# Hyperedge keys from one-hot matrix products, two node scores from one product, and the second node ordering made in layer 2

## The chip, the core and the metric

One core of a Trainium2 chip runs the whole program. The time is device microseconds (us) of one execution. The engines named below are TensorE (PE; its weight loads are listed apart as PEld), VectorE (DVE), ScalarE (ACT), GpSimd (POOL) and the queue of SyncE (SP), which issues most of the transfers.

## The reference

Four graph layers follow each other, each as `x = x + layer(relu(layernorm(x)))`, on `x` of 8 batches, 2048 nodes and 64 features, with one 2048x2048 matrix `adj` of zeros and ones. The change touches layer 0 and the preparation for layer 3:

```python
# layer 0 (h is the normalized input; H: 2048 nodes x 64 hyperedges, zeros and ones)
h = x @ W
s = leaky_relu(h @ a_node, 0.2)
alpha = softmax(where(H.T > 0, s, NEG), axis=-1)
agg = einsum('ben,bnf->bef', alpha, h)                      # one row per hyperedge
beta = sigmoid((h @ a_gn)[:, None, :] + (agg @ a_ge)[:, :, None])
all_he = elu(beta * h + (1 - beta) * agg)                   # one row per (hyperedge, node)
industry = einsum('nm,bmf->bnf', adj / deg, x @ W_ind)
g = einsum('bne,benf->bnf', softmax(where(H > 0, scores(elu(agg)), NEG)), all_he)
out = mix of industry and g by a two-way softmax
# layer 1: adj @ h and adj @ (adj @ h); layer 2: three times adj @ v with two small products
# layer 3 (graph attention over the neighbours that adj names)
e = adj * leaky_relu(e_src[:, None] + e_dst[None, :], 0.2)
h_prime = softmax(e) @ h
```

## The kernel before

Features stand as pairs of batches (4 pairs, `NP`), 128 nodes to a tile (16 tiles, `NT`), 512 nodes to a chunk (4 chunks, `NC`). Large SBUF areas are named slots, q0 to q9, of 16 KB a partition; who holds a slot decides when the next holder may write it. The source order of the instructions gives priorities, and a planner then fixes one order per engine from estimated times; each engine executes its own list strictly in that order. So a line that stands later in the source can run between earlier ones, but an instruction that waits holds up everything behind it on its engine.

`start` does the first layer norm, `h = x @ W` in both layouts (`h_t` by feature in q2 and q3, `h_n` by node in q4 and q5), and checks `adj`. `count_nodes` counts each node's hyperedges and neighbours, and writes both counts to DRAM (`degs`). A flag is then read, and a branch ends this part: nothing of what follows starts before it.

`layer0_pairs` follows. Nodes are ordered by how many hyperedges they have (fullest first), so that the j-th hyperedge of a node has to be worked on for few node tiles only.

- `hyperedge_keys` calls `sort_nodes` for that order. `sort_nodes` reads the counts back from DRAM, forms one class per count (`classes`, L340), counts with two small products (`pk`, `pb`), runs a prefix sum on VectorE (L412), gets each node's rank (L423), and inverts the ranks to an order with 16 steps of three VectorE instructions (L439, L443, L447) and a small product `pp` each. Then 16 indirect transfers of GpSimd (L498) fetch the rows of `H` in that order; they are transposed (L509), and a product with a triangle of ones gives `key`: for each hyperedge and node the running number of this hyperedge among the node's. Last, `sort_nodes` is called a second time, for the order by neighbours, which only layer 2's `neighbours` and layer 3 use.
- `aggregate` writes `h_n` to the DRAM table `h_rows` (L743), computes `h @ a_gn` with 128 TensorE instructions of two columns (`pb`, from L747) and writes that to `h_rows` as well (`hb`, L749 and L750). It computes the scores of `a_node` (`pl`, L759), loads `HT` to form `cap` (L767 to L769), and then for each of the four pairs: masked scores `logits` (L778), their maximum (L780), the exponential (L782), 16 transposes (L789), the product with `h_n` (`pa`), and a chain of small steps for the hyperedge's own scores. `logits` has two tiles, in q6 and q7, with two pairs each; `cap` and `score` are in q8, the fetched rows in q9.
- `x_ind` makes `x @ W_ind` as a high and a low part (L201, L202), nodes 0 to 1023 in q6 (high) and q8 (low), the others in q7 and q9.
- `adj_product` with `Pairs` then streams `adj` through TensorE and does the pairwise work beside it; `Pairs` fetches rows of `h_rows` by the order (L1738).

In layer 2 three products with `adj` are streamed; beside the first one `neighbours` finds each node's neighbours. It is a generator: `after` advances it once in every second step of the stream. It loads the order (L1473), fetches rows of `adj` (L1486) and works on them with VectorE instructions of 2048 elements (L1490, L1494, L1500, L1503). What is left of it is run before the third product.

Of the kernel before, what the change touches and what calls it, by code (L numbers as in the profile page):

```python
# [7 lines left out]
F = mybir.dt.float32  # L8
BF = mybir.dt.bfloat16

F12 = mybir.dt.float32r
I32 = mybir.dt.int32
# [7 lines left out]
P = 128  # L20
# [47 lines left out]

class Halves:
# [17 lines left out]
class Split:  # L87


    def __init__(self, slots, name):  # L90
        self.hi = Halves(slots, f"{name}_hi", ("q6", "q7"), True)
        self.lo = Halves(slots, f"{name}_lo", ("q8", "q9"), True)
        self.parts = self.hi, self.lo


class Kernel:
# [8 lines left out]
    def __init__(self, tc, ctx, a):  # L105
        self.tc, self.nc, self.a = tc, tc.nc, a
        self.flip = 0
        self.short = False
        self.consts = ctx.enter_context(tc.tile_pool(reuse_waits="tile", name="consts", bufs=1))

        dram = ctx.enter_context(tc.tile_pool(reuse_waits="tile", name="dram", bufs=1, space=bass.MemoryType.DRAM))
        self.xs = [
            [a["xT"][:, :, c * CW : (c + 1) * CW].rearrange("q p n -> p q n") for c in range(NC)]
        ]


        self.h_rows = dram.tile([N, ROW], F, name="h_rows")
        self.g_rows = dram.tile([N, NB * D], F, name="g_rows")
        self.degs = dram.tile([P, 2, NT], F, name="degs")
        self.orders = [dram.tile([P, 2, NT], I32, name=f"order{i}") for i in range(2)]  # L120


        self.f_rows = dram.tile([N, WIDE], F, name="f_rows")
        self.att_rows = dram.tile([N, NB * D], F, name="att_rows")
        self.rdeg = dram.tile([NT, P], F, name="rdeg")

        self.h_sums = [dram.tile([8, P, CW], F, name=f"sums{q}") for q in range(NP)]
        self.h_parts = [dram.tile([P, 3, N], BF, name=f"parts{q}") for q in range(NP)]
        for i in range(3):
            self.xs.append([dram.tile([P, NP, CW], F, name=f"x{i}_{c}") for c in range(NC)])  # L130
        self.setup()
# [211 lines left out]
    def count_nodes(self, pool, slots, adj_deg):  # L343


# [4 lines left out]
        deg = pool.tile([P, 2, NT], F, name="both_deg")  # L350
        nc.vector.tensor_reduce(deg[:, 0], hm, axis=AX.X, op=OP.add)
        nc.vector.tensor_copy(deg[:, 1], adj_deg)
        nc.sync.dma_start(self.degs, deg)
# [27 lines left out]
    def sort_nodes(self, w, ps, which, J, spare):  # L381

# [3 lines left out]
        deg = w.tile([P, NT], F, name="deg")  # L386
        nc.sync.dma_start(deg, self.degs[:, which])
        least = self.classes(w, deg, J)
# [9 lines left out]
        pk = ps.tile([P, K * NT], F, name="pk", tag="sort")  # L398
        self.mm(pk, ones, cls.rearrange(flat))
        pb = ps.tile([P, K * NT], F, name="pb", tag="sort")  # L400
# [4 lines left out]
        size = K * NT  # L405
        sums = [w.tile([P, left + size], F, name="sums"), spare[:, : left + size]]
# [19 lines left out]
        order = w.tile([P, 2, NT], I32, name="order")  # L426
        nc.vector.tensor_copy(order[:, 0], rank)

# [6 lines left out]
        linef, ownf = self.numbers(w, P)  # L435
        pp = ps.tile([P, 2 * NT], F, name="pp", tag="sort")
        for t in range(NT):
            here = w.tile([P, P], BF, name="here", bufs=2)
            nc.vector.tensor_scalar(  # L439
                here, linef, lowf[:, 1, t : t + 1], None, op0=OP.is_equal  # L440
            )
            ids = w.tile([P, 2, NT], BF, name="ids", bufs=2)
            nc.vector.tensor_scalar(  # L443
                ids[:, 0], linef[:, :NT], lowf[:, 0, t : t + 1], float(t), op0=OP.is_equal,
                op1=OP.mult,
            )
            nc.vector.tensor_scalar(  # L447
                ids[:, 1], linef[:, :NT], lowf[:, 0, t : t + 1], ownf, op0=OP.is_equal,
                op1=OP.mult,
            )  # L450
            self.mm(
                pp, here, ids.rearrange("p i t -> p (i t)"), start=t == 0, stop=t == NT - 1
            )
        perm = w.tile([P, 2, NT], F, name="permf")
        nc.vector.tensor_copy(perm.rearrange("p i t -> p (i t)"), pp)
# [4 lines left out]
        nc.sync.dma_start(self.orders[which], order)  # L460
        return order
# [24 lines left out]
    def hyperedge_keys(self, w, ps, slots, key):  # L486


        nc = self.nc
        both = slots.tile([P, 2, NT, 2 * D], F, name="twice", tag="q9")  # L490
        got = both[:, 0].rearrange("p t e -> p (t e)")
        got, spare = got[:, : NT * D], got[:, NT * D :]
        got = got.rearrange("p (t e) -> p t e", t=NT)
        order = self.sort_nodes(w, ps, 0, len(HELD) - 1, spare)

        twice = both[:, 1].rearrange("p t (s e) -> p t s e", s=2)
        for t in range(NT):
            nc.gpsimd.indirect_dma_start(  # L498
                got[:, t], None, self.a["H"],
                bass.IndirectOffsetOnAxis(ap=order[:, 1, t : t + 1], axis=0),  # L500
            )
        for i in range(2):
            nc.vector.tensor_scalar(twice[:, :, i], got, 0.0, None, op0=OP.is_gt)
        upto = self.upto(w)
        nc.vector.memset(upto[:D, D:], 0.0)
        for c in range(NC):
            pt = ps.tile([P, TC, P], F, name="pt", tag="sort")
            for i in range(TC):
                nc.tensor.transpose(  # L509
                    pt[:, i], twice[:, c * TC + i].rearrange("n s e -> n (s e)"), self.ident  # L510
                )
            mt = w.tile([P, CW], BF, name="mt", bufs=2)
            self.copy(mt, pt.rearrange("e i n -> e (i n)"))
            pc = ps.tile([P, CW], F, name="pc", tag="sort")
            self.mm(pc, upto, mt)
            nc.vector.tensor_mul(key[:, c * CW : (c + 1) * CW], pc, mt)
        self.sort_nodes(w, ps, 1, NEAR[1], spare)
        return order

    def start(self, pool, slots):  # L520

        nc, tc, a = self.nc, self.tc, self.a
        with tc.tile_pool(reuse_waits="tile", name="k00", bufs=1) as k:
# [48 lines left out]
    def x_ind(self, slots, k):  # L572
        w_ind = self.block_diag(k, self.a["W_ind"], "w_ind")
        x_ind = Split(slots, "x_ind")
        hn = self.h[0]
        with self.tc.tile_pool(reuse_waits="tile", name="x_ps", bufs=3, space=PSUM) as ps:
            for t in range(NT):
                pn = ps.tile([P, NP, P], F, name="pn")
                for q in range(NP):
                    self.mm(pn[:, q], hn(q)[:, t * P : (t + 1) * P], w_ind)  # L580
                self.split(x_ind, t, pn.rearrange("n q f -> n (q f)"))
        return x_ind
# [82 lines left out]
    def layer0_pairs(self, slots):  # L665
# [3 lines left out]
        with tc.tile_pool(reuse_waits="tile", name="k0", bufs=1) as k:  # L669
            fcw, av = self.scorer(k)  # L670
            ind = Halves(slots, "ind", ("q0", "q1"), False)
            with tc.tile_pool(reuse_waits="tile", name="k1", bufs=1) as k1:
# [6 lines left out]
                with (  # L679
# [3 lines left out]
                    self.hyperedge_keys(kw, kps, slots, key)  # L683
                    self.aggregate(slots, h_t, h_n, fcw, av, both, agg_hi, agg_lo)
                order = k1.tile([P, 2, NT], I32, name="order")
                nc.sync.dma_start(order, self.orders[0])
# [20 lines left out]
            order = k.tile([P, 2, NT], I32, name="order")  # L707
            nc.sync.dma_start(order, self.orders[0])
# [17 lines left out]
    def aggregate(self, slots, h_t, h_n, fcw, av, both, agg_hi, agg_lo):  # L726
        nc, tc, a = self.nc, self.tc, self.a
        with (
# [5 lines left out]
            agn = w.tile([P, 2], F, name="agn", bufs=1)  # L734
            node = w.tile([P, R], F, name="node", bufs=1)
            nc.vector.memset(agn, 0.0)
            nc.vector.memset(node, 0.0)
            for s in range(2):
                h = slice(s * D, (s + 1) * D)
                nc.vector.tensor_copy(agn[h, s : s + 1], self.col("a_gn")[h])  # L740
                nc.vector.tensor_copy(node[h, s : s + 1], self.col("a_node")[h])
            for t in range(NT):
                nc.sync.dma_start(self.h_rows[t * P : (t + 1) * P, : NB * D], h_n(t))  # L743
            pb = ps1.tile([P, NT, NB], F, name="pb", tag="pg")
            for t in range(NT):
                for q in range(NP):
                    self.mm(pb[:, t, 2 * q : 2 * q + 2], h_t(q)[:, t * P : (t + 1) * P], agn)  # L747
            hb = w.tile([P, NT, NB], F, name="hb", bufs=1)
            nc.vector.tensor_copy(hb, pb)  # L749
            nc.sync.dma_start(  # L750
                self.h_rows[:, NB * D :].rearrange("(t p) b -> p t b", p=P), hb
            )
# [3 lines left out]
            for ch in range(NC):  # L756
# [6 lines left out]
                )  # L763

            logits = [slots.tile([P, 2, N], F, name=f"logits{i}", tag=f"q{6 + i}") for i in range(2)]
# [6 lines left out]
            for q in range(NP):  # L772
                lg = logits[q // 2][:, q % 2]
# [55 lines left out]
                for s in range(2):  # L829
# [4 lines left out]
                    )  # L834
            flat = aggs.rearrange("p q s f -> p (q s f)")
# [535 lines left out]
    def layer2(self, slots):  # L1371
# [4 lines left out]
        with (  # L1376
# [41 lines left out]
            near = self.neighbours(k, slots) if self.short else iter(())  # L1418
# [48 lines left out]
    def neighbours(self, k, slots):  # L1467
# [5 lines left out]
        nc.sync.dma_start(order, self.orders[1])  # L1473
# [437 lines left out]
class Near:  # L1911
# [5 lines left out]
    def __init__(self, kern, slots, w, ps):  # L1917
# [15 lines left out]
        nc.sync.dma_start(self.order, kern.orders[1])  # L1933
# [323 lines left out]
```

## Time and profile before

| | |
|---|---|
| median of 3 runs | 2223.89 us (2223.14 to 2229.41) |
| the profiled execution | 2223.47 us, its span 2221.7 us |
| granted TensorE clock, mean | 0.905 |
| PE busy | 1967.9 us (89%) |
| DVE busy | 1115.2 us (50%) |
| ACT busy | 708.9 us (32%) |
| POOL busy | 727.9 us (33%) |

The span goes from the first to the last instruction of the profiled execution. Seen from its start, the first part ends at about 112 us with the branch; the keys and `aggregate` fill 112 to 270 us; the first product with `adj` and the pairs 270 to 484 us; the mix of layer 0 to 668 us; layer 1 to about 1385 us; layer 2 to about 1925 us; layer 3 the rest. Busy shares over the whole span average stages with different limits, so the stage from 112 to 270 us has to be read by itself. In lists of waits, "A <- B: 27.3, 1, 27.3" says that A stood idle 27.3 us in total, once, until B released it.

### The profile page before, as it was taken

The numbers are of one execution on the slowest core, as the hardware profiler recorded it, in microseconds if no ns is written. First come the engines' busy times: TensorE is split into PE (matmuls) and PEld (weight loads), VectorE is DVE, ScalarE is ACT, GpSimd is POOL, SyncE is SP. The second block draws the span as 40 slices with busy tenths as digits, with TensorE's granted clock in tenths as the row PEclk, the third lists the DMA queues.
The fourth block names the chain that finished last, engine by engine and source line by source line (L and its number), as shares of the span: only waits on it lengthen the run. The fifth ranks groups of instructions, "written<-read, shape, count | busy, mean of one in ns | idle before, by whom it ended". The sixth has DMA issues, their size and how long they took to land.

```text
span 2221.7 us, 21410 instructions
## 1 busy us (share of the span) xinstructions
PE 1967.9 (89%) x7530; PEld 1187.1 (53%) x7530; DVE 1115.2 (50%) x1980; ACT 708.9 (32%) x1347; POOL 727.9 (33%) x609
## 2 busy tenths in 40 slices
PE   5877899987879989999999998998999999679873
PEld 1454766652226766353353532876777666345432
DVE  7846767744762032524425244988302222349762
ACT  6401455543444342020110200433434333258300
POOL 0012066755320002726537175011000000277760
PEclk8856899996777989999999998999999999789996
DMA  8231133451122453040130402456333443375655
GB/s 318 71 101 27 52 94 112 126 159 67 38 76 86 131 130 118 0 139 13 54 99 0 114 1 82 149 191 218 103 123 123 144 151 124 131 199 164 180 158 201
DMA packets 107742, 253.76 MB, mean 114 GB/s; under 512 B 19600, under 2 KB 19744, under 8 KB 100320
## 3 DMA queue, kind: packets, MB, share of 16 engines
q1 hardware_dynamic: 90000, 185.22, 26.1%
q0 software_dynamic: 17616, 67.00, 10.1%
q8 instruction: 63, 1.03, 0.2%
q14 instruction: 63, 0.52, 0.1%
HBM read 218.37 MB, written 33.81 MB: 114 GB/s over the span
## 4 chain that ended last, share of the span: by engine, by line
PE 57%; DVE 8%; POOL 7%; DMA 6%; issue 5%; ACT 3%; SPq 1%; POOLq 0%; DVEq 0%; ACTq 0%
PE pp L135 25%; PE pk L135 16%; PE bank L135 4%; POOL ring L1959 3%; PE acc L135 3%; PE pn L135 2%; PE p L135 2%; POOL q L1794 1%; DVE q L1809 1%; DMA q<-in_adj_dram,order 1%; POOL dt L632 1%; DMA adj_t<-in_adjT_dram 1%; PE pd L135 1%; PE po L135 1%; DMA ring<-f_rows,near 1%
## 5 line engine op out<-in xcount | busy, mean ns | idle before, releaser
L294 ACT CAST adj<-adj_t 128x512 fp32r<-128x512 f32 x384 | 236.7, 619 | 718.3 <-PE pp L135 625.2
L1353 POOL TENSOR_TENSOR acc<-acc,y 128x512 f32<-128x512 f32 x224 | 277.4, 1271 | 444.9 <-DVE y L1348 444.9
L135 PE MATMUL pk<-q,w 128*128 128x512 f32 (+1 forms) x1024 | 358.2, 612 | 9.9 <-DVE w L1270 8.9
L135 PEld LDWEIGHTS pk<-q,w 128*128 128x128 f32 (+1 forms) x1024 | 136.6, 188 | 228.0 <-issue 179.1
L135 PE MATMUL acc<-q,ident 128*128 128x512 f32 x416 | 205.1, 620 | 30.0 <-DVE q L2049 19.1
L1348 DVE SCALAR_TENSOR_TENSOR y<-pk,bias,q 128x512 f32<-128x512 f32 x224 | 157.7, 746 | 139.9 <-PE pk L135 130.3
L135 PE MATMUL pp<-adj,u_n_hi 128*128 128x512 f32 x768 | 217.2, 402 | 0.0
L135 PE MATMUL pp<-adj,u_n_lo 128*128 128x512 f32 x768 | 214.2, 398 | 0.0
L135 PEld LDWEIGHTS pp<-adj,u_n_hi 128*128 128x128 f32 x768 | 143.4, 188 | 39.0 <-issue 5.9
L1959 POOL DMA_INDIRECT ring<-f_rows,near x121 | 141.4, 1169 | 69.2 <-issue 57.4
L135 PEld LDWEIGHTS pp<-adj,u_n_lo 128*128 128x128 f32 x768 | 144.6, 188 | 34.5
L135 PEld LDWEIGHTS acc<-q,ident 128*128 128x128 f32 x416 | 77.1, 196 | 106.3 <-issue 48.8
L2063 POOL IOTA q<- 128x2048 int32 x1 | 1.8, 1835 | 355.3 <-PE p L135 355.3
L1794 POOL TENSOR_TENSOR q<-q,beta 128x512 f32<-128x512 f32 x57 | 67.6, 1188 | 104.8 <-DVE beta L1770 81.6
L135 PE MATMUL pp<-adj,x_ind_hi 128*128 128x512 f32 x256 | 95.5, 489 | 2.1 <-DVE q L700 1.9
L1348 DVE SCALAR_TENSOR_TENSOR acc<-pk,bias,q 128x512 f32<-128x512 f32 x32 | 22.6, 746 | 143.6 <-PE pk L135 143.6
L135 PE MATMUL bank<-std,from_rows 32*128 32x512 f32 x128 | 47.7, 938 | 41.8 <-DVE std L242 33.8
L135 PE MATMUL pp<-adj,h_n_hi 128*128 128x512 f32 x256 | 77.7, 416 | 0.0
L135 PE MATMUL pp<-adj,h_n_lo 128*128 128x512 f32 x256 | 75.3, 407 | 0.0
L2030 DVE TENSOR_TENSOR q<-ring,e 128x1024 f32<-128x1024 f32 x58 | 69.9, 1217 | 9.9 <-PE acc L135 9.7
L135 PE MATMUL pp<-adj,ah_n_hi 128*128 128x512 f32 x256 | 73.1, 405 | 0.0
L1416 DVE TENSOR_TENSOR q<-pn,later 128x512 f32<-128x512 f32 x32 | 21.5, 687 | 101.6 <-PE pn L135 101.4
(382 smaller groups left out, 3216.7 us busy)
## 6 DMA issues: line engine op xcount, KB each, us to landing
adj_t<-in_adjT_dram SPq DMA_DIRECT2D x160, 512.0 KB, 3.8
rows<-in_adj_dram SPq DMA_DIRECT2D x16, 1024.0 KB, 5.6
adj_t<-in_adjT_dram SPq DMA_DIRECT2D x64, 256.0 KB, 3.0
q<-x SPq DMA_DIRECT2D x12, 1024.0 KB, 5.0
q<-in_embT_dram SPq DMA_DIRECT2D x8, 1024.0 KB, 12.2
x<-q SPq DMA_DIRECT2D x8, 1024.0 KB, 3.9
x_ch<-in_xT_dram SPq DMA_DIRECT2D x4, 1024.0 KB, 6.2
h_rows<-q SPq DMA_DIRECT2D x16, 256.0 KB, 2.9
```

The source lines that it names most:

```text
L135: self.nc.tensor.matmul(out, lhsT, rhs, start=start, stop=stop)
L294: nc.scalar.copy(moving, at[:, i])
L632: nc.gpsimd.tensor_sub(dt, th[0], th[1])
L1348: nc.vector.scalar_tensor_tensor(y, pks[b, half], bias[:, b : b + 1], emb[:, b], op0=OP.add, op1=OP.mult,)
L1353: nc.gpsimd.tensor_add(acc, acc, y)
L1416: nc.vector.tensor_add(to, pn, later[:, 2].unsqueeze(1).to_broadcast(full))
L1794: self.nc.gpsimd.tensor_tensor(x, x, by.unsqueeze(2).to_broadcast([P, NB, D]), op=OP.mult)
L1809: nc.vector.tensor_add(d, d, self.pas.pop(i - 1))
L1959: self.nc.gpsimd.indirect_dma_start(to, None, self.kern.f_rows[:], bass.IndirectOffsetOnAxis(ap=index, axis=0))
L2030: nc.vector.tensor_tensor(y.rearrange("n i (b f) -> n i b f", b=NB), block[:, i : i + 2, : NB * D].rearrange("n i (b f) -> n i b f", b=NB) ...
L2063: nc.gpsimd.iota(whole, pattern=[[1, N]], base=0, channel_multiplier=0)
```

## The change

The hyperedge counts stay in SBUF (`self.deg`), and the transfer to DRAM and back is gone. `sort_nodes` is split: `ranks` ends with the ranks, `by_rank` inverts them, now with whole-tile VectorE instructions (`here`, `place`, `ids`) followed by 16 products. `hyperedge_keys` no longer fetches rows: it loads `H` in node order with one transfer and, for each chunk of 512 places and each of 16 node tiles, makes a one-hot matrix (`hot`: which node has this rank) and multiplies. The products put the columns in order, so the transposes are gone too. It has become a generator, advanced once after each pair of `aggregate`; the order itself is made after the second pair.

`h @ a_gn` comes out of the same product as the scores of `a_node` (two more columns of `node`); the product is copied to `raw` by ScalarE, and after each pair four tiles of it are transposed and the wanted columns copied to `hb`, which is written to `h_rows` after the fourth pair. `logits` has one tile now, in q6, used by turns; `raw` and the rank's working space take q7; `x_ind`'s first nodes stand in q7 (high) and q9 (low).

The order by neighbours is made in layer 2, by `ranks` and `by_rank` at the head of `neighbours`, in the slot q4, with the PSUM banks called `p2`; it is written to DRAM for layer 3.

```diff
-        nc.sync.dma_start(self.degs, deg)
...
-    def sort_nodes(self, w, ps, which, J, spare):
+    def ranks(self, w, bank, which, J):
...
-        deg = w.tile([P, NT], F, name="deg")
-        nc.sync.dma_start(deg, self.degs[:, which])
-        least = self.classes(w, deg, J)
+        least = self.classes(w, self.deg[:, which], J)
...
+        return rank
+
+    def by_rank(self, w, bank, rank, order):
...
+        nc.vector.tensor_tensor(
+            here, line.unsqueeze(1).to_broadcast(full), lowf[:, 1].unsqueeze(2).to_broadcast(full),
+            op=OP.is_equal,
+        )
...
+        nc.vector.tensor_mul(ids[:, 0], place, tiles.unsqueeze(2).to_broadcast(full))
+        nc.vector.tensor_scalar(ids[:, 1], place, own, None, op0=OP.mult)
...
         for t in range(NT):
-            here = w.tile([P, P], BF, name="here", bufs=2)
-            nc.vector.tensor_scalar(
-                here, linef, lowf[:, 1, t : t + 1], None, op0=OP.is_equal
-            )
-            ids = w.tile([P, 2, NT], BF, name="ids", bufs=2)
...
+            self.mm(pp, here[:, t], ids[:, :, t], start=t == 0, stop=t == NT - 1)
...
-    def hyperedge_keys(self, w, ps, slots, key):
+    def hyperedge_keys(self, w, bank, both, rank, key):
...
-        order = self.sort_nodes(w, ps, 0, len(HELD) - 1, spare)
...
-        for t in range(NT):
-            nc.gpsimd.indirect_dma_start(
-                got[:, t], None, self.a["H"],
-                bass.IndirectOffsetOnAxis(ap=order[:, 1, t : t + 1], axis=0),
-            )
+        nc.sync.dma_start(got, self.a["H"].rearrange("(t p) e -> p t e", p=P))
...
+        line, _ = self.numbers(w, CW)
         for c in range(NC):
-            pt = ps.tile([P, TC, P], F, name="pt", tag="sort")
-            for i in range(TC):
-                nc.tensor.transpose(
-                    pt[:, i], twice[:, c * TC + i].rearrange("n s e -> n (s e)"), self.ident
+            here = w.tile([P, NT], F, name="rank_here", bufs=2)
+            nc.vector.tensor_scalar(here, rank, float(-c * CW), None, op0=OP.add)
+            pt = bank()
+            for t in range(NT):
+                hot = w.tile([P, CW], BF, name="hot", bufs=4)
+                nc.vector.tensor_scalar(hot, line, here[:, t : t + 1], None, op0=OP.is_equal)
+                self.mm(
+                    pt, twice[:, t].rearrange("n s e -> n (s e)"), hot, start=t == 0,
+                    stop=t == NT - 1,
                 )
...
             nc.vector.tensor_mul(key[:, c * CW : (c + 1) * CW], pc, mt)
-        self.sort_nodes(w, ps, 1, NEAR[1], spare)
-        return order
+            yield
...
-        x_ind = Split(slots, "x_ind")
+        x_ind = Split(slots, "x_ind", ("q7", "q6", "q9", "q8"))
...
-                    self.hyperedge_keys(kw, kps, slots, key)
-                    self.aggregate(slots, h_t, h_n, fcw, av, both, agg_hi, agg_lo)
-                order = k1.tile([P, 2, NT], I32, name="order")
-                nc.sync.dma_start(order, self.orders[0])
...
+                    rank = self.ranks(Parts(raw[:, 1]), bank, 0, len(HELD) - 1)
+                    keys = self.hyperedge_keys(kw, bank, twice, rank, key)
+                    for i, _ in enumerate(
+                        self.aggregate(slots, raw[:, 0], h_t, h_n, fcw, av, both, agg_hi, agg_lo)
+                    ):
+                        next(keys, None)
+                        if i == 1:
+                            self.by_rank(Parts(twice[:, 0]), bank, rank, order)
...
+                nc.vector.tensor_copy(node[h, 2 + s : 3 + s], self.col("a_gn")[h])
             for t in range(NT):
                 nc.sync.dma_start(self.h_rows[t * P : (t + 1) * P, : NB * D], h_n(t))
-            pb = ps1.tile([P, NT, NB], F, name="pb", tag="pg")
-            for t in range(NT):
-                for q in range(NP):
-                    self.mm(pb[:, t, 2 * q : 2 * q + 2], h_t(q)[:, t * P : (t + 1) * P], agn)
...
+                nc.scalar.copy(raw[:, s], pl)
+
+            logits = slots.tile([P, 2, N], F, name="logits", tag="q6")
...
+                g = q
+                pt = ps1.tile([P, 4, P], F, name="pt")
+                for i in range(4):
+                    t = 4 * g + i
+                    nc.tensor.transpose(pt[:, i], raw[:, t * P : (t + 1) * P], self.ident)
+                nc.vector.tensor_copy(
+                    hb[:, 4 * g : 4 * g + 4].rearrange("n i (q s) -> n i q s", s=2),
+                    pt.rearrange("n i (q c) -> n i q c", c=R)[:, :, :, 2:4],
+                )
+                yield
+            nc.sync.dma_start(
+                self.h_rows[:, NB * D :].rearrange("(t p) b -> p t b", p=P), hb
+            )
...
-        nc.sync.dma_start(order, self.orders[1])
+        w = Parts(slots.tile([P, 2 * N], F, name="sort", tag="q4"))
+        rank = self.ranks(w, bank, 1, NEAR[1])
+        yield
+        self.by_rank(w, bank, rank, order)
+        nc.sync.dma_start(self.order3, order)
+        yield
```

## The prediction

> **What bounds the kernel now.** I read the 40 slices of the page first. TensorE is nine tenths busy nearly everywhere, but in the third to fifth slice (111 to 278 us) it is not, and its granted clock is at half.
>
> ```profile
> ## 2 busy tenths in 40 slices
> PE   5877899987879989999999998998999999679873
> DVE  7846767744762032524425244988302222349762
> PEclk8856899996777989999999998999999999789996
> ```
>
> Then busy time in stretches of that stage. Columns: stretch, its length, then busy time and count of PE, PEld, DVE, ACT, POOL; then clock, DMA share, GB/s.
>
> ```profile
> 113.60:141.00 27.40, 27.40 (x129) 27.38 (x130) 0.17 (x2) 0.00 (x0) 0.00 (x0) 0.50 0.11 40
> 161.00:174.50 13.50, 13.50 (x28) 3.75 (x27) 8.79 (x10) 2.48 (x3) 10.76 (x10) 0.50 0.15 27
> 174.50:185.30 10.80, 0.09 (x2) 0.03 (x1) 1.75 (x4) 2.09 (x2) 8.06 (x10) 0.50 0.18 46
> 197.00:216.00 19.00, 16.75 (x98) 13.04 (x97) 16.25 (x39) 4.94 (x9) 0.29 (x1) 0.90 0.00 0
> 216.00:230.00 14.00, 8.19 (x40) 5.36 (x41) 13.10 (x57) 2.68 (x3) 0.00 (x0) 0.68 0.00 1
> 254.00:268.80 14.80, 12.62 (x111) 12.25 (x109) 11.52 (x39) 9.35 (x19) 0.00 (x0) 1.00 0.32 96
> ```
>
> The reader should see three holes: 27.4 us in which TensorE alone works, 10.8 us in which it does nothing while GpSimd issues fetches, and 216 to 230, where it idles half the time beside a full VectorE. The waits of 112 to 270 us, and those of the SP queue, name them:
>
> ```profile
> DVE hb L749 <- PE pb L135: 27.3, 1, 27.3
> PE pt L509 <- DVE twice L503: 10.7, 1, 10.7
> DVE twice L503 <- DMA twice<-in_H_dram,order: 9.1, 1, 9.1
> PE pp L135 <- DVE ids L447: 13.8, 28, 4.0
> SPq L387 <- DVE cls L391: 27.0, 1, 27.0
> ```
>
> So VectorE stands behind `hb` until the 128 small products end; the SP queue stands behind the second load of counts (L387) with 12 of 16 `h_rows` writes and both `HT` loads; TensorE later waits for fetched rows. Last, groups of VectorE and the stretches of layer 2:
>
> ```profile
> L439 DVE TENSOR_SCALAR here<-linef,lowf 128x128 bf16<-128x128 f32 x32 | 8.9, 278 | 0.7 <-PE pp L135 0.7
> L143 DVE COPY et<-pt 128x512 f32<-128x512 f32 x8 | 5.5, 688 | 3.4 <-PE pt L789 3.4
> 1411.00:1559.00 148.00, 139.41 (x616) 109.30 (x615) 132.62 (x95) 50.11 (x84) 21.30 (x13) 0.98 0.59 200
> 1572.00:1709.00 137.00, 136.77 (x615) 107.31 (x613) 13.33 (x20) 49.62 (x84) 0.00 (x0) 1.00 0.41 126
> ```
>
> **The change part by part.** All sums are against the profiled execution (2223.47 us, span 2221.7), 0.4 us under the median 2223.89: the same for this purpose. The stage begins at 113.6 and ends with the first product with `adj` at 269.8.
>
> *Up to the first masked scores (L778 at 167.2).* The 128 products (27.4 us) go. What is late next is `cap`: its mask (L768) starts at 161.26 as the second `HT` load lands. From the SP queue's resuming `h_rows` writes at 142.9 that took 18.4 us (12 writes of 0.61, two issues, 7.2 to land). Without the count loads the queue goes straight on: four writes (1.8 us) from 113.9, then 18.4, so L768 at about 134, L769, and L778 at 136.5 instead of 167.2. The scores are earlier: the 32 `pl` instructions take 8.9 us at half clock, to about 123, then the sign steps. Four ScalarE copies to `raw` (0.60 each) and one more load of `H` (0.43 us issue; the same load in the first part landed in 6.8) lie beside this. Ranks: 13 classes, eight additions of about 0.4 and the rest, some 8 us of VectorE, done near 125. **Gain 30.7.**
>
> *The hole at 174.5.* The 16 fetches (1.25 us apart on GpSimd, 160.7 to 182.3) and the wait on them go: **gain 10.7.** The load of `H` in node order replaces them 10 us before it is needed.
>
> *The middle, 185.3 to 254 (68.7 us).* Out: the second sort. VectorE: nine additions (4.0), at, rank, copies (3.5), 16 x 0.53 for the inversion (8.5), together 16 us; TensorE's idle half of 216 to 230 (5.8) and 16 transposes of rows (4.3). In: 64 one-hots and 64 products. The row for a one-hot is L439: started every 0.20 us for 128 columns, while L443 beside it, 16 columns, is started every 0.14; 112 columns cost 0.06, so 512 cost 0.20 + 384 x 0.06/112 = 0.40, 25.6 us for 64. [...] Some 20 of the 64 fit between 125 and 136.5, where VectorE would wait for `cap`; 44 are left, 17.6 us against 16 taken out. Inverting the first sort by whole tiles costs about 4 us instead of 8.5.
>
> On TensorE a product of 512 columns is started every 0.233 us at full clock (the stream's groups of four, 0.93 apart). [...] The trace shows 0.50 through 174.5 and 0.68 to 0.90 after 197. At 0.5 the 64 products cost 29.8 us, at full clock 14.9[...]. I take 0.8, 18.6, 44 of them here: 12.8. Four tiles of `raw` per pair add 16 transposes (2.4) and four short copies (1). TensorE: +15.2 - 4.3 - 3 (the second sort's `pp`) = +8, less the 5.8 of idleness. **Loss 2**, between a gain of 8 (warm clock: the 59 us of TensorE work here shrink) and a loss of 20 [...].
>
> *The tail, 254 to 269.8.* 80 of the 128 `x_ind` products lie here now, 48 before. With q7 under `raw` and q9 under the keys, none can start until the last transposes of `raw` and the last key product: 48 x 0.118 = 5.7 us more here, of which I let 3 come back in the middle. `hb` is now written at the end: copy 0.3, issue 0.6, landing 4.9, fetch 0.95 and 3.8, 10.5 us, beside 15.1 us of `x_ind` and 2.9 of `pb`. It costs nothing while these last; with no cover, up to 10. **Loss 3.**
>
> *Layer 2.* Sort and inversion come to 10 + 4.5 us of VectorE, and cannot start before 1385.2 (slot q4 is read until then). The neighbours' chain, with VectorE 90% busy to 1559 and ending at 1571.6, moves back by some 25 us; the third product, which needs it finished, begins at 1709: 137 us of cover. It needs 58 advances of the generator plus two; the stream offers 64. GpSimd's fetches wait behind the order, and nothing else is queued there. TensorE gets 18 small products (2 x 0.3, 16 x 0.19 = 3.6), and could stand behind the chain at two places, up to 10 us. No row shows this wait; the same products on TensorE's list waited 13.8 us in 28 pieces before because `ids` came one by one. **Loss 3**, between 1 and 14.
>
> The warm clock deserves a term of its own: pairs' `pl` (22.7 us for 32 instructions, mean 863 ns) run at 0.50 for the first two pairs; fewer holes should return **5**, between 0 and 10.
>
> Sum: 30.7 + 10.7 - 2 - 3 - 3 + 5 = 38.4. 2223.5 - 38.4 = 2185. The pairs, the mix, layer 1 and layer 3 have the same instructions, only earlier.
>
> **The rivals.** *The keys come last.* The source places chunk c after pair c; if the planner keeps them there, the early one-hots (8 us) are not early, chunk 3 (6.4 + 2) stands before `x_ind`, and nothing of the 5 or the 3 returns. That takes about 20: 2205. For it: the planner's order of the first sort left VectorE behind `hb` for 27 us. Against: in 145 to 160 it mixed two sorts well.
>
> *The stage becomes compact.* TensorE's work in it, at full clock, is 75 to 85 us; if the idle shares vanish, it ends 55 us earlier: 2168. For it: the 0.50 rows; against: the chain of each pair (a reduction of 2.3, an exponential of 2.2, transposes, small steps).
>
> *Lock step (slower).* Each product needs its one-hot and each one-hot a free buffer of four; with both engines strictly in order, a late instruction of the pair's chain stops both. [...] The gains without the keys' cost are 30.7 + 10.7 + 16 + 5 = 62, less 6 for tail and layer 2: 56. From 0.87 us per one-hot nothing is left[...]. Against: four buffers, and the `here` and `pp` of the first sort ran at VectorE's pace, 0.53 us, with no hand-over on top.
>
> *It does not do what it says* would be a fetch still waited for: the pairs still gather rows of `h_rows`, now behind `hb`; uncovered, that is 10 less gain, 2195, inside the range.
>
> **How the numbers follow.** The forecast with its bounds 0.68; keys last 0.15; compact 0.10; no change that can be measured 0.02; lock step 0.05. About 0.3%, 6.7 us, is what a measurement of this kernel can tell from none. Faster 0.93, same 0.02, slower 0.05. The range reaches from compact (2166) to keys last (2207).
>
> **What would show it.** Right: L778 first near 136; no wait of DVE on `pb` and no L498; 64 one-hots of about 0.48 us duration; first product with `adj` near 229; the neighbours' last L1507 near 1597, and the third product begun no later relative to layer 2's start than before plus 3. Wrong: one-hots of 0.7 us, TensorE waiting on `hot` by more than 10 us in sum, `x_ind` alone at the end for over 20 us, or a hole in layer 2's stream.

## The result, and the profile after

The changed kernel takes 2192.55 us (median of 5 runs, 2190.21 to 2206.33) against 2223.89: a ratio of 0.9868, 95% interval 0.9838 to 0.9898, some 31 us faster. The forecast was 2185, in a range of 2166 to 2207. The sign and the largest term were right; the gain is some 7 us smaller than the sum said.

Three rows of the 40 slices of the changed kernel, in tenths, as shown for the kernel before:

```profile
## 2 busy tenths in 40 slices
PE   5869999978879979999999998999999999679883
DVE  7877677725651133525434245898602222349772
PEclk8868999977759989999999998999999999789986
```

The granted clock of the third slice was 5 tenths and is 6, that of the fourth was 6 and is 8. TensorE's busy share in the third is still only six tenths. Busy time in stretches of this stage (columns: stretch, length, busy time and count of PE, PEld, DVE, ACT, POOL; clock, DMA share, GB/s):

```profile
113.60:141.00 27.40, 13.53 (x46) 3.40 (x47) 19.76 (x55) 4.51 (x8) 1.16 (x6) 0.62 0.69 214
123.00:135.00 12.00, 2.49 (x4) 0.58 (x4) 5.25 (x12) 1.34 (x3) 0.00 (x0) 0.61 0.80 205
135.00:148.00 13.00, 12.04 (x19) 3.88 (x21) 11.91 (x22) 3.38 (x3) 0.32 (x2) 0.50 0.00 1
148.00:165.00 17.00, 16.64 (x85) 10.14 (x85) 15.88 (x39) 4.81 (x9) 0.00 (x0) 0.90 0.00 1
165.00:185.00 20.00, 19.95 (x103) 12.06 (x103) 16.46 (x41) 4.47 (x9) 0.00 (x0) 0.76 0.00 1
185.00:204.00 19.00, 15.79 (x84) 10.22 (x84) 15.64 (x37) 5.04 (x9) 0.00 (x0) 0.86 0.00 0
217.00:238.00 21.00, 19.60 (x152) 19.14 (x152) 13.80 (x40) 11.70 (x22) 2.79 (x3) 0.90 0.46 155
```

Of the three holes of before, the one in which TensorE alone did small products and the one behind the fetches are gone. A new one stands at 123 to 135: TensorE does 2.5 us of work in 12 and VectorE 5.3, while the DMA engines are 80% busy. Then, up to 204, both engines are busy for eight tenths of the time or more. The waits of 112 to 217 us, and that of VectorE's one-hots in the groups of the stage (its line has the total busy time, the mean ns of one, then the idle time before and its releaser), say what for:

```profile
DVE cap L779 <- DMA cap<-in_HT_dram: 6.6, 1, 6.6
PE pl L153 <- DVE logits L789: 9.1, 1, 9.1
PE bank L153 <- DVE hot L519: 3.2, 2, 2.9
L519 DVE TENSOR_SCALAR hot<-linef,rank_here 128x512 bf16<-128x512 f32 x64 | 28.0, 481 | 2.6 <-PE bank L153 2.3
```

VectorE stands for `HT`, whose load is issued at 122.6, behind the 16 writes of `h_rows` (4 MB, issued from 113.4 on); TensorE stands for the masked scores. No wait on the small products or on fetched rows is left. VectorE's timeline over the hole (start, duration, what, [idle before]):

```profile
124.22 1.27 DVE L519 TENSOR_SCALAR hot<-linef,rank_here 128x512 bf16<-128x512 f32 x3
132.11 1.23 DVE L779 TENSOR_SCALAR cap<-cap 128x2048 f32<-128x2048 f32 x1 [6.62 <-DMA cap<-in_HT_dram]
134.69 1.29 DVE L789 TENSOR_TENSOR logits<-pl,cap 128x512 f32<-128x512 f32 x2
135.90 1.28 DVE L509 TENSOR_SCALAR twice<-twice 128x1024 bf16<-128x1024 f32 x2
```

Four one-hots are made before the hole (the first at 123.22) and none in it: the four buffers of `hot` are full, and no product can empty one, because the other factor, `twice`, is made from `H` only at 135.9. The load of `H` stands behind both loads of `HT` in the same queue: it is issued at 123.8 and takes 9.6 us to land, so it is not there before about 133.4 either. The end of the stage on TensorE (the last line is that of the kernel before):

```profile
216.62 16.91 PE L153 MATMUL pn<-w_ind,q 128*128 128x128 f32 x126
...
238.18 1.74 PE L153 MATMUL pp<-adj,x_ind_hi 128*128 128x512 f32 x4
...
269.76 1.91 PE L135 MATMUL pp<-adj,x_ind_hi 128*128 128x512 f32 x4
```

The first product with `adj` (the "stage end" from here on) begins at 238.2 instead of 269.8.

### The profile page after: what moved, and what is told of

It is laid out like the page before. It is cut to its first block, busy times and chain, and to the rows that moved or that the text cites. A ratio compares the mean times of both kernels' runs of the same rounds, so it can differ in the third digit from the quotient of the medians.

```text
span 2204.5 us, 21222 instructions
## 1 busy us (share of the span) xinstructions
PE 1961.8 (89%) x7461; PEld 1166.3 (53%) x7466; DVE 1135.3 (52%) x1964; ACT 713.0 (32%) x1351; POOL 709.2 (32%) x595
## 4 chain that ended last, share of the span: by engine, by line
PE 55%; DVE 11%; POOL 7%; issue 6%; DMA 5%; ACT 3%; SPq 1%; POOLq 0%; DVEq 0%; ACTq 0%
PE pp L153 23%; PE pk L153 16%; PE bank L153 4%; PE acc L153 3%; POOL ring L1991 2%; PE p L153 2%; PE pn L153 2%; DMA q<-in_adj_dram,order 1%; POOL q L1826 1%; DVE q L1841 1%; POOL dt L644 1%; DVE top L1532 1%; PE pd L153 1%; PE po L153 1%; PE pt L1252 1%
## 5 line engine op out<-in xcount | busy, mean ns | idle before, releaser
L1518 POOL DMA_INDIRECT q<-in_adj_dram,order x15 | 21.9, 1459 | 174.9 <-DVE top L1532 136.0
L2062 DVE TENSOR_TENSOR q<-ring,e 128x1024 f32<-128x1024 f32 x58 | 70.1, 1220 | 11.5 <-PE acc L153 11.3
```

Of the source, the lines that this page charges most:

```text
L1518: nc.gpsimd.indirect_dma_start(row, None, self.a["adj"], bass.IndirectOffsetOnAxis(ap=order[:, 1, t : t + 1], axis=0),)
L2062: nc.vector.tensor_tensor(y.rearrange("n i (b f) -> n i b f", b=NB), block[:, i : i + 2, : NB * D].rearrange("n i (b f) -> n i b f", b=NB) ...
```

## The experiments

All kernels ran in turn with the kernel before, which gave medians of 2223.7 to 2225.8 in these sets; a median here is that of 4 to 12 executions. The stage's end in the trace is the sharper measure: in the two profiles of the change it differs by 0.6 us, while from there to the end of the span the profiled executions took anything from 1946 to 1966 us with nearly the same instructions. Where the intervals of two kernels overlap, their medians alone do not tell them apart. That is so for e4_usort, e5_ukeys, e7_tmm and e8_half beside e1_again, for e9_fetch and e10_loads16 beside e2_loads, and for e12_smallloads beside e3_usmall.

| kernel | first masked scores | stage end | median, us | ratio to before (95%) |
|---|---|---|---|---|
| before | 167.2 | 269.8 | 2223.89 | |
| the change, first profile | 134.7 | 238.2 | 2192.55 | 0.9868 (0.9838 to 0.9898) |
| e1_again | 135.0 | 238.8 | 2191.55 | 0.9855 (0.9835 to 0.9876) |
| e2_loads | 128.2 | 229.2 | 2183.11 | 0.9810 (0.9786 to 0.9834) |
| e3_usmall | 157.4 | 260.3 | 2216.14 | 0.9959 (0.9941 to 0.9977) |
| e12_smallloads | 154.9 | 259.1 | 2210.09 | 0.9935 (0.9911 to 0.9959) |
| e4_usort | 139.4 | 243.3 | 2195.55 | 0.9868 (0.9847 to 0.9890) |
| e5_ukeys | 133.6 | 235.1 | 2189.92 | 0.9846 (0.9812 to 0.9880) |
| e6_thot | 133.6 | 260.2 | 2214.97 | 0.9957 (0.9940 to 0.9974) |
| e7_tmm | 133.7 | 237.8 | 2199.25 | 0.9872 (0.9838 to 0.9906) |
| e8_half | 132.8 | 236.4 | 2185.95 | 0.9834 (0.9805 to 0.9864) |
| e9_fetch | 128.0 | 221.0 | 2177.36 | 0.9791 (0.9770 to 0.9811) |
| e10_loads16 | 127.3 | 224.8 | 2177.77 | 0.9792 (0.9768 to 0.9816) |
| e11_best16 | 127.4 | 226.8 | 2185.90 | 0.9840 (0.9817 to 0.9863) |

**The change again.**

> The changed kernel unaltered, for a second profile. In the first, layer 1 (from the clock's dip at 1012 us to 1365) took 353 us against 345 before the change, with the same instructions. Theory 'a slow execution': layer 1 takes 345 to 347 here, the profiled execution is near 2195, the median 2190 to 2195. Rival 'the change slows layer 1': 352 to 354 again, and some 8 us of gain are still to be had.

From stage end to the head of layer 2 (its first TensorE instruction) it took 1117 us here, 1116 in the kernel before, 1127 in the first profile of the change. The extra 10 us there, and 9 more behind it, belong to that one execution (its 2206.33 us is the slowest of its five), not to the change. Differences to the change are taken from this run.

**Loads first.** The two loads of `HT` and that of `H` are issued ahead of the writes:

```diff
+            for s in range(2):
+                nc.sync.dma_start(cap[s * D : (s + 1) * D], a["HT"])
             for ch in range(NC):
...
             logits = slots.tile([P, 2, N], F, name="logits", tag="q6")
-            for s in range(2):
-                nc.sync.dma_start(cap[s * D : (s + 1) * D], a["HT"])
+            for t in range(NT):
+                nc.sync.dma_start(self.h_rows[t * P : (t + 1) * P, : NB * D], h_n(t))
```

> One thing moved: the load of H and the two of HT are issued on the SP queue ahead of the 16 writes of h_rows (4 MB), which follow the scores. Theory 'the failed step of the early one-hots is a matter of the queue': the masks L779 start near 123 instead of 132.1, the first masked scores near 126, one-hots and products run in the 9 us for which TensorE stood; first product with adj near 229 instead of 238, median 2181 to 2185. Rival 'the middle is full anyway': the masks come early, but the end of the stage moves by under 3 us (2189 or more). Second rival 'the writes come back': the writes of h_rows, now behind, land late and the pairs' first fetch waits; then L1762's stretch starts no earlier, 2190 to 2200.

VectorE's timeline:

```profile
124.51 0.69 DVE L774 SCALAR_TENSOR_TENSOR cap<-pl,cap 128x512 f32<-128x512 f32 x1 [0.83 <-ACT cap L773]
125.12 1.22 DVE L782 TENSOR_SCALAR cap<-cap 128x2048 f32<-128x2048 f32 x1
```

The masks now follow the scores without a wait. The stage ends 9.5 us earlier (6.8 of them are there at the first masked scores), the median falls by 8.4; the queue theory holds. One detail differs from the expectation: only two one-hots are made ahead of the first masked scores, because VectorE is busy with scores and masks until then; what was saved is the idle time. The second rival fails: no engine but the SP queue (2.6 us in all) is seen to wait for the writes that now stand behind the loads.

**The small products back.** The 128 two-column products return, `raw`, its copies and transposes go:

```diff
-                nc.vector.tensor_copy(node[h, 2 + s : 3 + s], self.col("a_gn")[h])
+                nc.vector.tensor_copy(agn[h, s : s + 1], self.col("a_gn")[h])
...
+            for t in range(NT):
+                for q in range(NP):
+                    self.mm(pb[:, t, 2 * q : 2 * q + 2], h_t(q)[:, t * P : (t + 1) * P], agn)
...
-                nc.scalar.copy(raw[:, s], pl)
```

> One part undone: h @ a_gn by 128 products of two columns again, with hb copied and written at once; the copies to raw and its 16 transposes are gone. Theory 'front': 27.4 us of TensorE at half clock stand before the scores; 19 us of waiting for loads absorb 12 of it; 2.4 us of transposes return: +14, 2202 to 2210, first masked scores near 150. Rival 'hidden by the wait for cap': the scores go first and the products lie beside the loads: +5 or less, 2192 to 2197. Second rival: the clock stays at half for longer, the whole +27: 2217.

It costs 24.6 us, by its number close to the second rival. TensorE's timeline and the SP queue's wait:

```profile
117.32 27.47 PE L153 MATMUL pb<-agn,q 128*128 128x2 f32 x128
...
SPq L770 <- DVE linef L496: 23.4, 1, 23.4
```

The scores stand behind the products, but the queue also stands 23.4 us behind the writing of `hb`, with the loads of `HT` after it, so the run alone does not say which of the two sets the price. The same kernel with the loads of `HT` and `H` first does:

> e3_usmall (the 128 small products back) with the loads of HT and H moved ahead of the writes of h_rows. In e3_usmall the loads of HT stood 23.4 us on the SP queue behind the writing of hb, and the masks began only at 154.8. Theory 'TensorE's 27.4 us are the price': the masks come near 125 now, but the scores still wait for the products, which end near 145; first masked scores 151 to 153, stage end near 255 against 260.3, median 2208 to 2213. Rival 'the queue was the price': first masked scores by 140, median 2190 to 2200.

```profile
116.80 27.47 PE L153 MATMUL pb<-agn,q 128*128 128x2 f32 x128
151.25 0.69 DVE L786 SCALAR_TENSOR_TENSOR cap<-pl,cap 128x512 f32<-128x512 f32 x1
154.91 1.28 DVE L801 TENSOR_TENSOR logits<-pl,cap 128x512 f32<-128x512 f32 x2
259.09 1.91 PE L153 MATMUL pp<-adj,x_ind_hi 128*128 128x512 f32 x4
```

`HT` is there in time, and the first masked scores still come at 154.9: TensorE's time is the price, and not the queue. The median is where that theory put it; the first masked scores come 2 us and the stage's end 4 us later than it said. The pair that differs by this part alone, with the loads first in both, is e12_smallloads and e2_loads, whose first product with `adj` is

```profile
229.22 1.91 PE L153 MATMUL pp<-adj,x_ind_hi 128*128 128x512 f32 x4
```

So the part costs 29.9 us in the stage's end and 27.0 in the median: about the whole 27.5 us for which the products hold TensorE. With the loads late it cost 21.5 and 24.6.

**The second sort back in layer 0**, ahead of the scores:

```diff
+                    rank3 = self.ranks(ww, bank, 1, NEAR[1])
+                    order3 = kw.tile([P, 2, NT], I32, name="order3")
+                    self.by_rank(ww, bank, rank3, order3)
...
-        rank = self.ranks(w, bank, 1, NEAR[1])
-        yield
-        self.by_rank(w, bank, rank, order)
+        nc.sync.dma_start(order, self.order3)
```

> One part undone: the second sort (its ranks and its inversion by whole tiles, some 14.5 us of VectorE) stands ahead of the scores of layer 0 again, and its order is loaded in the third layer. Theory 'on the path': 6.6 us of waiting for cap absorb some of it, 8 remain, and layer 2 gives 1 back: 2197 to 2201, first masked scores near 143. Rival 'hidden behind the loads': within 2 us of the changed kernel. Second rival 'layer 2 paid more than the trace shows': faster by 3 or more, 2188 or less.

It costs 4.0 us in the median and 4.5 in the stage's end, just short of the first theory. Of the 14.5 us, 6.6 fill VectorE's wait for `HT`, which is gone from this trace; where the other 3 to 4 went is not traced. Layer 2, from its head to the end of the second product, takes 324.4 us here, 324.4 before the change and 325.6 in e1_again.

**Keys from fetched rows.**

```diff
-                nc.vector.tensor_scalar(hot, line, here[:, t : t + 1], None, op0=OP.is_equal)
...
+        for t in range(NT):
+            nc.gpsimd.indirect_dma_start(
+                got[:, t], None, self.a["H"],
+                bass.IndirectOffsetOnAxis(ap=rank[:, 1, t : t + 1], axis=0),
+            )
```

> One part undone: the keys are made from rows of H fetched by 16 indirect DMAs and turned by 16 transposes, ahead of the pairs; the inversion of the first sort comes first, since the fetches need it; the 64 one-hots and 64 products are gone. Theory of the prediction (a hole of 10.7 us saved against 17.6 us of one-hots late in the middle, 4.3 of transposes back): the hole returns, the middle becomes shorter, and the sum is within 4 us of the changed kernel, 2188 to 2196. Rival 'the hole is the larger': the fetches, 1.25 us apart on GpSimd behind the inversion at 127, land at 150, TensorE stands 10 us or more, and the middle wins little because VectorE's chain sets it: 2198 to 2206. Rival 'the middle is full of one-hots': faster than the changed kernel by over 6, 2185 or less.

The waits of the stage, and two stretches of it:

```profile
PE bank L519 <- DVE twice L513: 16.1, 1, 16.1
123.00:148.00 25.00, 9.37 (x36) 2.41 (x28) 8.75 (x14) 2.37 (x4) 13.86 (x14) 0.57 0.35 91
185.00:204.00 19.00, 18.96 (x124) 14.56 (x124) 11.97 (x24) 7.69 (x14) 0.00 (x0) 0.95 0.00 1
```

TensorE stands for the rows by 16.1 us, more than before the change, and still the stage ends 3.6 us earlier than in e1_again; the medians differ by 1.6. With the rest of the change in place, this part of it gains nothing: what the hole cost is paid in one-hots. In 185 to 204 VectorE is busy 12 us instead of 15.6, and TensorE is full at 0.95.

**What sets the middle.** Each one-hot made twice, each product done twice (with one-hots valued 0.5, so that the sum is the same), and the row of numbers in fp16 (parts of the three edits, in this order):

```diff
+                nc.vector.tensor_scalar(hot, line, here[:, t : t + 1], None, op0=OP.is_equal)
...
+                for j in range(2):
+                    self.mm(
+                        pt, twice[:, t].rearrange("n s e -> n (s e)"), hot,
+                        start=t == 0 and j == 0, stop=t == NT - 1 and j == 1,
+                    )
...
+        line = w.tile([P, CW], mybir.dt.float16, name="line16")
+        nc.vector.tensor_copy(line, line32)
```

> Every one-hot is made twice on VectorE (64 more instructions of 0.40 us, 25.6 us); nothing else changes. Theory 'VectorE sets the middle': of 60 late ones some 20 to 24 us show in the first product with adj (258 to 262) and in the time, 2211 to 2216. Rival 'TensorE and the chain of each pair set it': the additions lie beside products and exponentials, +8 or less, 2200 or less.

> Every product of the keys is done twice with one-hots valued 0.5 (64 more products, 0.23 us each at full clock, 0.30 at the granted 0.75 to 0.9: 15 to 19 us of TensorE); VectorE's instructions stay 64. Theory 'VectorE sets the middle': +6 or less, 2198 or less, and part of it only where the pair's own products wait. Rival 'TensorE sets it': +14 to +19, 2206 to 2211. Between them (+7 to +13): both are full in turns, as the stretches of the changed kernel say (TensorE 19.95 of 20 us in 165 to 185, VectorE 15.9 of 17 in 148 to 165).

> The row of numbers 0 to 511 that the one-hots are compared with is kept as fp16 (whole numbers to 2048 are exact) instead of float32; the rank stays float32. What a one-hot of 512 columns then costs is not shown by any trace: between the 0.40 us from start to start that it takes now and half of it. Theory 'VectorE sets the middle and 16-bit operands are faster': 0.25 to 0.28 us, 8 us of VectorE less, 5 to 8 us of the time, 2184 to 2187. Rival 'the duration is that of the element count or of the scalar operand': 0.40 again, 2190 to 2193. Rival 'faster, but VectorE does not set it': 0.26 us and under 2 us of gain.

First the same two stretches of e1_again (lines 1 and 2) and of e7_tmm (3 and 4), then the one-hots of e8_half (481 ns each in the change), and the first product with `adj` of e1_again, e6_thot, e7_tmm and e8_half:

```profile
165.00:185.00 20.00, 20.00 (x103) 12.09 (x102) 16.51 (x42) 4.92 (x12) 0.00 (x0) 0.76 0.00 1
185.00:204.00 19.00, 15.85 (x84) 10.13 (x84) 15.55 (x37) 5.04 (x9) 0.00 (x0) 0.86 0.00 0
165.00:185.00 20.00, 19.84 (x121) 12.25 (x124) 16.48 (x43) 4.93 (x10) 0.00 (x0) 1.00 0.00 1
185.00:204.00 19.00, 17.66 (x105) 10.90 (x105) 15.86 (x38) 5.04 (x9) 0.00 (x0) 1.00 0.01 1
...
L521 DVE TENSOR_SCALAR hot<-line,rank_here 128x512 bf16<-128x512 f16 x64 | 20.0, 349 | 3.4 <-PE bank L153 2.5
...
238.75 1.70 PE L153 MATMUL pp<-adj,x_ind_hi 128*128 128x512 f32 x4
260.20 1.40 PE L153 MATMUL pp<-adj,x_ind_hi 128*128 128x512 f32 x4
237.80 1.91 PE L153 MATMUL pp<-adj,x_ind_hi 128*128 128x512 f32 x4
236.42 1.75 PE L153 MATMUL pp<-adj,x_ind_hi 128*128 128x512 f32 x4
```

Of 25.6 us added to VectorE, 21.5 show in the stage's end and 23.4 in the median. Of 64 products added to TensorE nothing shows in the stage's end (237.8): TensorE is hardly busier by time, since it is granted the full clock where it had 0.76 and 0.86. VectorE's work sets the middle, though it is not busy all the time there (16.5 of 20 us); TensorE's "20.00 of 20" was work at a lower clock with room in it. The median of e7_tmm is still 7.7 above e1_again, which by itself lies in the band between the two theories, though the intervals overlap. In its profile 1963 us follow the stage's end against 1947, in stages with the same instructions, as in the first profile of the change. Why some executions have this is open, so that the doubled products cost no time is shown for the stage, not for the whole kernel. With fp16 a one-hot starts every 0.27 us instead of 0.40, 8.3 us less for 64; the stage ends 2.3 earlier and the median is 5.6 lower. So adding to VectorE costs nearly its whole length and taking away gives part of it. With the loads first the same edit gives 4.4 (e10_loads16 below), so the wait for the loads takes some of it; what takes the rest, perhaps the pair's own chain, is not shown.

**Better versions.** e9_fetch keeps e2_loads, fetches rows right behind the first sort's inversion, and does a chunk of their transposes after each pair; e10_loads16 joins e2_loads and e8_half; e11_best16 adds ScalarE for all `et` and `mt` copies (the last two lines below):

```diff
+                    self.by_rank(Parts(kw.tile([P, N], F, name="sort")), bank, rank, order)
+                    for t in range(NT):
+                        nc.gpsimd.indirect_dma_start(
+                            twice[:, 0, t * D : (t + 1) * D], None, a["H"],
+                            bass.IndirectOffsetOnAxis(ap=order[:, 1, t : t + 1], axis=0),
+                        )
...
-                    self.copy(et[:, 4 * g : 4 * g + 4], pt)
+                    nc.scalar.copy(et[:, 4 * g : 4 * g + 4], pt)
```

> A third way to the keys, on top of e2_loads: rows of H are fetched in sorted order as before the change (16 indirect DMAs right behind the inversion of the first sort), but the transposes of a chunk stand after a pair's work, as the one-hot products do in the changed kernel, so that the fetches lie beside the first pair. Theory 'the gain at the keys came from where they stand, not from the one-hots': no wait of TensorE on the rows above 3 us, VectorE freed of 24.6 us of late one-hots. The price of a VectorE microsecond in the middle is bracketed by e6_thot (21.5 us later for 25.6 added: 0.84) and e8_half (2.3 earlier for 8.4 taken away: 0.27), so the stage ends 7 to 20 us before e2_loads's 229.2: 209 to 222, median 2162 to 2177. Rival 'the fetch cannot be hidden': TensorE stands for the rows again by 8 us or more and the time is that of e2_loads or above, 2183 or more.

> e2_loads and e8_half together (early loads, fp16 numbers). Theory 'with the loads early VectorE is what is late, so that cheaper one-hots now count': they add up or better, first product with adj 222 to 227, median 2175 to 2179. Rival 'the chain of each pair is the floor': no more than e2_loads, 2181 to 2184.

> e10_loads16, with all copies of exponentials (et) and of key rows (mt) on ScalarE, which has 7 us of work in a pair of 18: VectorE loses another 8 copies or so of 0.69. Theory 'VectorE is late': 2 to 5 us better than e10_loads16. Rival 'the copies are in the pair's chain, and one engine doing them in turn is no slower and no faster': within 2 us of it. Rival 'ScalarE stands behind its own long exponential': 2 us or more worse.

The waits and one stretch of e9_fetch, and its last `x_ind` products:

```profile
PE bank L514 <- DVE twice L508: 1.8, 1, 1.8
140.00:158.00 18.00, 16.20 (x49) 9.82 (x47) 6.57 (x10) 3.27 (x4) 11.32 (x13) 0.55 0.12 25
206.62 9.68 PE L153 MATMUL pn<-w_ind,q 128*128 128x128 f32 x80
```

The fetches (GpSimd busy 11.3 us in the second line) lie beside the first pair; TensorE stands for the rows 1.8 us instead of 16.1. The stage ends at 221.0, 8.2 us before e2_loads, at the near end of the expectation (the median lies 0.4 us outside it), and 48 of the 128 `x_ind` products slip into the middle again. At 2177.36 us it beats the kernel before and the change. e10_loads16 is as fast, at 2177.77: early loads and cheaper one-hots add up (the stage ends 4.4 us before that of e2_loads, the median is 5.3 lower). e11_best16 is worse, by its numbers what its last rival said (that rival's cause is not shown): its stage ends 2.0 us later than e10_loads16's, and its median is 8.1 us higher, with intervals that just do not overlap. Its runs lie between 2174.69 and 2194.40, and the profiled one is the fastest, so where the other 6 us arise is open. In the stage VectorE now stands longer for the product `pa`, which needs the copies (e10_loads16, then e11_best16):

```profile
DVE aggs L816 <- PE pa L153: 5.2, 3, 2.6
DVE aggs L816 <- PE pa L153: 13.3, 4, 5.2
```

## Why the prediction was right, and where its sum was off

*Up to the first masked scores*: 30.7 us forecast, 32.5 measured. The cause is the one named: the small products go (e3_usmall and e12_smallloads), and `HT` is late next.

*The hole at 174.5*: gone, as said; but with the rows fetched again (e5_ukeys) the time is the same. The forecast had it so in its terms, 10.7 gained and 17.6 of late one-hots paid; it set the second sort's 16 us of VectorE against the one-hots. e4_usort does not test that credit: it puts the sort ahead of the scores, where it costs only 4, and not into the middle, where the kernel before had it. By e6_thot's price (21.5 for 25.6 us of VectorE) 16 us there would be worth 13, an estimate that no run tests.

*The middle, a loss of 2*: this step failed. "Some 20 of the 64 fit between 125 and 136.5" overlooked the factor `twice`: the load of `H` was put "10 us before it is needed", though the queue issues it behind 16 writes and two loads. Four were early; 16 x 0.40 = 6.4 us came later. e2_loads removes the idle time and with it 9.5 us. The price of a one-hot was right: 0.40 us, estimated from the row of before. The "loss of 20" that the step allowed was the author's estimate for a slower one-hot, which no trace shows. Six in a row in e2_loads take 2.46 us, the last of them 0.48, so they start (2.46 - 0.48) / 5 = 0.40 us apart:

```profile
190.69 2.46 DVE L518 TENSOR_SCALAR hot<-linef,rank_here 128x512 bf16<-128x512 f32 x6
```

*The clock, a gain of 5*: this step failed too. That "fewer holes" would bring a higher clock was the author's estimate, shown by no trace, and they did not: the 32 `pl` of the pairs took 22.7 us before and 22.5 in e1_again, and in 135 to 148, right after the new hole, the clock is 0.50, as in 161 to 174.5 before, although TensorE is busy 12.0 of 13 us (with the products doubled, in e7_tmm, it is 0.74 there, at 12.3 us busy). The forecast's own first row spoke against the step (27.40 us busy at 0.50), and of the three slices that it called half clock only the first was at 5 tenths; the others had 6 and 8. The 0.8 taken for the key products is about what the stretches show after that (0.76 to 0.90).

*The tail, a loss of 3*: of 5.7 us for 48 more `x_ind` products, 3 were to come back in the middle. In the change none do: all but two of the 128 stand at the end. `hb` was covered, as said: it is issued at 211.5 us and lands in 3.0, 24 us ahead of the stage's end.

*Layer 2, a loss of 3*: the last near copy (L1539) comes at 212.8 us after the head of layer 2 against 186.2 before, 26.6 later where 25 was said, and the cover holds: the stretch to the end of the second product is 1.3 us longer. The term was too large by about 2.

Together: 1.8 more at the front, 6.4, 5 and 3 less behind it make 228.4 + 12.6 = 241.0 for the stage's end; measured 238.2 and 238.8. The 2 to 3 us left over are not assigned to a step. For the whole kernel the corrected terms, layer 2 at 1.3, give a gain of 38.4 - 12.6 + 1.7 = 27.5 us, where the medians show 31.3, and 33.6 in the set of e1_again: some 4 to 6 us of the forecast's closeness are luck as far as is known, and its range of 41 us was wide enough for either. Of the rivals, "the keys come last" was half true: the early one-hots failed and the tail was whole, for a cause that it did not name. "The stage becomes compact" did not come: the stage went from 156 to 125 us, against 75 to 85 of TensorE's work at full clock (its "55 us earlier" does not follow from these figures). Lock step did not appear: TensorE waits for `hot` 3.2 us in all.

## What to carry to other kernels

Before work is placed into a wait, follow each operand back through its DMA queue: here the hole was a wait of 6.6 us for a load, and the filler's own load, which took 9.6 us to land, stood behind that one. To tell which engine sets a stage, add work to each in turn: here a TensorE that was busy 20.00 of 20 us, at a granted clock of 0.76, was not the bound (64 more products left the stage's end at 237.8, against 238.8). And when a slow fetch is replaced by computing, try first to start the fetch earlier: here the same fetch laid beside other work did as well (2177.36 us) as the best one-hots (2177.77).

## What was not expected of the hardware

With the key products doubled (e7_tmm) the granted clock was 1.00 in the two stretches where e1_again had 0.76 and 0.86, and 64 more products did not move the stage's end (237.8 against 238.8): TensorE was busy 77.9 us in 135 to 217 instead of 75.8. And the 128 two-column products hold TensorE busy without a gap for 27.4 us at a clock of 0.50 (the stretch of before that starts at 113.60; in e3_usmall and e12_smallloads they take 27.47 us). Being busy by time alone did not bring the full clock there. What does is not shown.
